# Layer 0: both adjacency mixes side by side, then both weight stages; each mix emptied by ScalarE and VectorE

## The chip, the cores and the metric

The kernel runs on one core of a Trainium2 chip. The metric is the device time of one execution in microseconds; the figure given is the median of several runs.

## The reference

Input x is 128 graphs of 64 nodes with 256 features, 8192 tokens in all; adj is one 64 by 64 adjacency matrix shared by all graphs. Four layers follow each other, each on a layer norm with a ReLU, each added to x. The change is in the first half of layer 0, two graph convolutions; the LSTM windows after them, and the layers 1 to 3 (attention, a normalised graph convolution, a three-step graph convolution) are not touched.

```python
h = jnp.maximum(_layernorm(x, axis=-1), 0.0)
# layer 0, up to the LSTM
h = relu(einsum('ts,bsh->bth', adj, h @ Wg0 + bg0))
h = relu(einsum('ts,bsh->bth', adj, h @ Wg1 + bg1))
```

## The kernel before

All data are float32. The tokens of layer 0 are worked off in 16 groups (`NG`) of 512 tokens (`GN`), each as four tiles of 128 tokens. The product with adj is taken before the product with the weights, so that a group passes through these stages:

- layer norm (`ln_relu`, L84 to L120): statistics on VectorE (L92, L94, L95), the power -1/2 on GpSimd (L96), a last small step on VectorE (L98), and four ScalarE instructions (L111) that write the normalised tile h.
- the first mix (`first_mix`, L428): 32 small matmuls of 64 by 64 (L145) multiply adj with h, into two PSUM banks. Two copies empty the banks into the tile m0: L158 and L453 are where they are issued.
- the first weights (`first_weights`, L480): 8 matmuls over the full array (L488) multiply m0 with the first weight matrix, into two banks. VectorE adds the bias (L496), GpSimd takes the ReLU (L497); the result is h1.
- the second mix (`second_mix`, L500): again 32 small matmuls (L145), adj with h1, into two banks; two copies (L158) fill m1.
- the second weights (`second_weights`, L505): 4 matmuls over the full array (L512), the weight matrix with m1, into two banks. For each of the two banks VectorE adds the bias (L517) and ScalarE writes the ReLU in a turned layout (L520) to the tile that the LSTM reads.

A matmul of float32 stands in the trace as two records. In the prediction mix1, W1, mix2 and W2 are these four stages on TensorE, T is the start of a mix1, and a number in brackets is a group's.

The groups overlap by a hand-written loop (L523 to L533). In iteration g, TensorE receives the first mix of group g, then the second weights of group g-2, then the second mix of group g-1, then the first weights of group g. In iteration 16 the second weights of group 14 are cut in two around the second mix of group 15. Each engine takes its own instructions in the order in which the tile framework's scheduler wrote them; they wait on each other by semaphores. Except for group 0, both copies of a first mix are on VectorE (`on_vector`, then `on_vector_last`), and both copies of a second mix are on ScalarE, except for the last one, which has one on each. The tiles h, m0, h1, m1 and s1 have two buffers each, x three; PSUM has eight banks, which all matmuls share in turn. `issue_after` puts an instruction behind another in the order: the statistics of a layer norm behind the copy of two groups ahead, its step L98 behind the copy of the group ahead.

The loads of x (L58) and of the LSTM's weights (L319) are issued from SyncE's queue. After the last group the LSTM begins; its matmuls are at L569.

Of the kernel before, what the change touches and what calls it, by code (L numbers as in the profile page):

```python
# [20 lines left out]
NG = NTOK // GN  # L21
# [17 lines left out]
def adj_preln_kernel(ctx: ExitStack, tc: tile.TileContext, x_in, adj, vec, bg0, bg1,  # L39
# [9 lines left out]
    def bank(shape=(P, 512)):  # L49
        return psp.tile(list(shape), F32, tag="ps", name="ps")  # L50
# [6 lines left out]
    def load_x(x, g):  # L57
        nc.sync.dma_start(out=x, in_=x_view[:, g * GT : (g + 1) * GT, :])  # L58
# [13 lines left out]
    adj2 = const.tile([P, NODES], F32, tag="adj2", name="adj2")  # L72
# [44 lines left out]
    def ln_relu(src, dst, between=None):  # L117

        rstd, nmr, _ = ln_scale(src, between)
        ln_apply(src, dst, rstd, nmr)  # L120
# [11 lines left out]
    def mix(src, a2, chunks, dst, copies, swap=False, banks=None, behind=lambda t, last: None,  # L132
            order=None):

        for c0, tiles in order or [(c0, range(GT)) for c0 in range(0, chunks, 2)]:
            pss = banks.pop(0) if banks else [bank((P, 2, GT, NODES)) for _ in range(2)]
            for t in tiles:
                for c in range(2):  # L140
                    for half in range(2):
                        for b in range(2):
                            rows = slice(b * 64, b * 64 + 64)
                            col = (c0 + c) * P + half * 64
                            last = nc.tensor.matmul(  # L145
                                pss[b][half * 64 : half * 64 + 64, c, t, :],
                                lhsT=src[rows, t, col : col + 64],
                                rhs=a2[rows, :],
                                start=True, stop=True,
                            )  # L150
                behind(t, last.ins)
            for b in range(2):
                if swap:
                    to = dst[:, c0 : c0 + 2, :].rearrange("p c (k b m) -> p b c k m", b=2, m=P)
                    last = copies[b](to[:, b], pss[b].rearrange("p c (k q) n -> p c k (q n)", q=2))
                else:
                    to = dst[:, c0 : c0 + 2, :].rearrange("p c (t b n) -> p b c t n", b=2, n=NODES)
                    last = copies[b](to[:, b], pss[b])  # L158
        return last.ins

    on_vector, on_scalar = nc.vector.tensor_copy, nc.scalar.copy
# [153 lines left out]
    with tc.tile_pool(name="lw", bufs=5) as lw:  # L315
# [6 lines left out]
        with tc.tile_pool(name="gw", bufs=1) as gw, tc.tile_pool(name="gcn", bufs=2) as gp, \  # L322
# [105 lines left out]
            def first_mix(g):  # L428
                nonlocal first_copied, first_scalar, turned, second_ln
                h = gp.tile([P, GT, D], F32, tag="h", name="h")  # L430
                if g == 0:
                    for k, (rstd, nmr, _) in enumerate(lns):
                        two = slice(2 * k, 2 * k + 2)
                        ln_apply(xs[0][:, two], h[:, two], rstd, nmr, 2, (1,) if k else ())
                elif g == 1:
                    with tc.issue_after(first_copied):
                        rstd, nmr, second_ln = ln_scale(xs[1])
                    with tc.issue_after(first_scalar):
                        ln_apply(xs[1], h, rstd, nmr)
                    with tc.issue_after(first_copied):  # L440
                        row_sums()
                else:
                    if g < NK:
                        x = xs[g]
                    else:
                        x = gp.tile([P, GT, D], F32, tag="x", name="x", bufs=3)
                        load_x(x, g)
                    with tc.issue_after(second_ln if g == 2 else copied_of[g - 2].ins):
                        ln_relu(x, h, lambda: copied_of[g - 1])
                m0 = gp.tile([P, 2, GN], F32, tag="m0", name="m0")  # L450

                def on_vector_last(*args):
                    copied_of.append(nc.vector.tensor_copy(*args))  # L453
                    return copied_of[-1]

                if g == 0:


                    def on_scalar_first(*args):
                        nonlocal first_scalar  # L460
                        last = nc.scalar.copy(*args)
                        first_scalar = last.ins
                        return last

                    copied = mix(h, adj2, 2, m0, (on_scalar_first, on_vector_last))
                    first_copied = copied
                    with tc.issue_after(copied):
                        nc.vector.tensor_scalar(rb0[:, 0, :], rb0[:, 0, :], rsum, None, ALU.mult)
                else:
                    copied = mix(h, adj2, 2, m0, (on_vector, on_vector_last))  # L470
                if g == NG // 4:

                    with tc.issue_after(copied):
                        adjacency_forms()
                        turned = normalized_adjacency()
                if g == NG // 2:
                    turned()
                return m0

            def first_weights(m0):  # L480

                h1 = gp.tile([P, GT, D], F32, tag="h1", name="h1")
                for k in range(2):
                    ps = bank((P, 2, D))
                    for t in range(2):
                        tok = (2 * k + t) * P
                        for c in range(2):
                            nc.tensor.matmul(  # L488
                                ps[:, t, :],
                                lhsT=m0[:, c, tok : tok + P],  # L490
                                rhs=wg[0][:, c, :],
                                start=(c == 0),
                                stop=(c == 1),
                            )
                    hk = h1[:, 2 * k : 2 * k + 2, :]
                    nc.vector.tensor_tensor(hk, ps, rb0.to_broadcast([P, 2, D]), ALU.add)  # L496
                    nc.gpsimd.tensor_scalar(hk, hk, 0.0, None, ALU.max)  # L497
                return h1

            def second_mix(h1, last):  # L500
                m1 = gp.tile([P, 2, GN], F32, tag="m1", name="m1")
                mix(h1, adj2, 2, m1, (on_scalar, on_vector if last else on_scalar))
                return m1

            def second_weights(g, m1, ms=range(2)):  # L505

                dst = hs[g // PER][:, :, :, (g % PER) * GB : (g % PER + 1) * GB]
                for m in ms:
                    ps = bank((P, GB, NODES))
                    pf = ps.rearrange("p b n -> p (b n)")  # L510
                    for c in range(2):
                        nc.tensor.matmul(  # L512
                            pf, lhsT=wg[1][:, c, m * P : (m + 1) * P], rhs=m1[:, c, :],
                            start=(c == 0), stop=(c == 1),
                        )
                    s1 = gp.tile([P, GB, NODES], F32, tag="s1", name="s1")
                    nc.vector.tensor_tensor(  # L517
                        s1, ps, rb1[:, m].to_broadcast([P, GB, NODES]), ALU.add
                    )
                    nc.scalar.activation(dst[:, m], s1.rearrange("p b n -> p n b"), AF.Relu)  # L520


            h1, m1 = None, None  # L523
            for g in range(NG + 2):
                if g < NG:
                    m0 = first_mix(g)
                before = m1
                if before is not None:
                    second_weights(g - 2, before, range(1 if g == NG else 2))
                m1 = second_mix(h1, g == NG) if h1 is not None else None  # L530
                if g == NG:
                    second_weights(g - 2, before, [1])
                h1 = first_weights(m0) if g < NG else None  # L533


        with tc.tile_pool(name="back", bufs=1, reuse_waits="tile") as back_pool, \
# [198 lines left out]
            for p, nk in ((1, 8), (2, 8), (3, 7), (4, 8)):  # L735
# [7 lines left out]
                for j in range(0, len(units), 2):  # L743
# [23 lines left out]
                    for t in range(1, p):  # L767
                        for i, u in enumerate(two):
# [21 lines left out]
                            if p == 4 and j == 2 and t == p - 1 and i == 0:  # L790

                                h = back_pool.tile([P, GT, D], F32, tag="hc", name="h")
# [59 lines left out]
    with tc.tile_pool(name="att", bufs=2, reuse_waits="tile") as ap_:  # L852
# [150 lines left out]
        last, put_down = None, None  # L1003
        for g in range(NG):
# [14 lines left out]
            if g == 0:  # L1019
                h = normalized(1)  # L1020
# [50 lines left out]
            last = (e_next[0], ri_next, v)  # L1071
            with tc.issue_after(sub):
# [4 lines left out]
                if g + 2 < NG:  # L1077
                    h = normalized(g + 2)
# [155 lines left out]
    for g in range(NG):  # L1234
# [20 lines left out]
        else:  # L1255
# [11 lines left out]
            def evicted(m):  # L1267
                return nc.scalar.copy(o[:, m, :], pss[m])

            for m in range(2):  # L1270
                nc.vector.bn_stats(st2[:, m, g, :], pss[m])
                if (g, m) != (NG - 1, 1):
                    last = evicted(m)
# [302 lines left out]
    for g in range(NG + 1):  # L1576
        if g == 0:
            bring(0, 3)
        if g < NG:

            m1 = arena(ar_right)
            h1, summed = first_weights(a, m1)
# [91 lines left out]
```

## Time and profile before

| what | value |
|---|---|
| median of 3 runs | 2445.6 us (2445.13 to 2445.6) |
| profiled execution: its time, its span | 2446.36 us, 2444.5 us |
| TensorE busy | 2425.3 us (99%) |
| VectorE, ScalarE, GpSimd busy | 1539.8, 1127.5, 463.9 us |
| granted TensorE clock | 0.999 |
| first matmul of the LSTM | starts at 162.96 us |

A profile shows one execution. Its busy times are sums over each engine, PE is TensorE's matmuls and PEld its weight loads, DVE is VectorE, ACT ScalarE, POOL GpSimd, SP SyncE. A line's bracket at its end gives the idle time of the engine before that instruction, and what ended it; "issue" is time in which it waited for nothing that the profile shows. L numbers are lines of the kernel's file. What happens up to 163 us is layer 0's two graph convolutions, 7% of the span; the rest is not part of the change.

### The profile page before, as it was taken

The page shows a single profiled execution, that of the slowest core. Times are in us where ns is not written, and L with a number is a line of the kernel's source. Part 1 is how long each engine was busy: PE and PEld are TensorE (multiplying, and loading weights), DVE is VectorE, ACT ScalarE, POOL GpSimd, SP SyncE. Part 2 cuts the span into 40 slices and gives each one's busy share as a digit, 9 for nine tenths or more (in the row PEclk, how much of TensorE's full clock was granted, in tenths as well). Part 3 has the DMA queues.
Part 4 walks back from the last instruction along what each step waited for, and adds up shares of the span by engine and source line. Part 5 has one row for each costly group of instructions (what it writes and reads, how often), then busy time and mean ns, then how long its engine had stood idle before and what let it go on. Part 6 is the DMA issues. An engine that isn't in the chain of part 4 may idle for free.

```text
span 2444.5 us, 46563 instructions
## 1 busy us (share of the span) xinstructions
PE 2425.3 (99%) x19564; PEld 2068.5 (85%) x19564; DVE 1539.8 (63%) x2752; ACT 1127.5 (46%) x2010; POOL 463.9 (19%) x400
## 2 busy tenths in 40 slices
PE   9999999999999999999999999999999999999999
PEld 6678888889999998888888864486988898898888
DVE  6668866666566675575599886476556445454544
ACT  4557754544444443353455566564333323333332
POOL 4432211111111111112224431023111111101110
PEclk9999999999999999999999999999999999999999
DMA  3200000001000000143246410010133100000000
GB/s 128 94 2 1 1 18 1 1 1 35 1 1 1 1 1 1 18 96 70 48 81 128 79 36 2 1 61 10 29 60 62 27 10 19 10 10 10 18 10 18
DMA packets 161585, 73.20 MB, mean 30 GB/s; under 512 B 104416, under 2 KB 157792, under 8 KB 161376
## 3 DMA queue, kind: packets, MB, share of 16 engines
q1 hardware_dynamic: 147712, 56.82, 9.5%
q0 software_dynamic: 12672, 12.58, 3.4%
q8 instruction: 154, 2.52, 0.4%
q10 hardware_dynamic: 992, 0.82, 0.1%
q14 instruction: 55, 0.45, 0.1%
HBM read 40.84 MB, written 20.97 MB: 25 GB/s over the span
## 4 chain that ended last, share of the span: by engine, by line
PE 91%; DVE 5%; ACT 2%; issue 1%; DMA 0%; POOL 0%; DVEq 0%; ACTq 0%; POOLq 0%
PE ps L569 41%; PE ps L1459 16%; PE ps L1507 8%; PE ps L831 4%; PE ps L1419 4%; PE ps L145 4%; PE ps L881 3%; PE ps L512 2%; PE ps L488 2%; PE ps L1211 2%; PE ps L1262 2%; PE ps L903 1%; PE ps L1528 1%; PE ps L964 1%; DVE e L947 1%
## 5 line engine op out<-in xcount | busy, mean ns | idle before, releaser
L569 PE MATMUL ps<-diff,s 128*128 128x256 f32 (+1 forms) x1824 | 393.5, 371 | 0.9 <-DVE diff L690 0.9
L1459 PE MATMUL ps<-arena 128*128 128x256 f32 x1792 | 393.3, 380 | 0.3 <-DVE arena L215 0.3
L1459 PEld LDWEIGHTS ps<-arena 128*128 128x128 f32 x1792 | 337.9, 190 | 55.1 <-issue 9.8
L569 PEld LDWEIGHTS ps<-diff,s 128*128 128x128 f32 x1824 | 345.9, 190 | 33.8 <-issue 1.6
L583 ACT ACTIVATE gates<-gates,lbias 128x512 f32<-128x512 f32 (+5 forms) x426 | 244.3, 621 | 200.5 <-DVE gates L194 144.4
L188 POOL TENSOR_TENSOR gates<-p 128x512 f32<-128x512 f32 (+1 forms) x115 | 148.6, 1292 | 882.0 <-DVE p L184 831.1
L569 PE MATMUL ps<-h,w 128*128 128x256 f32 (+1 forms) x1028 | 241.0, 371 | 0.0
L569 PE MATMUL ps<-diff,w 128*128 128x256 f32 (+1 forms) x1040 | 238.7, 370 | 0.0
L569 PEld LDWEIGHTS ps<-diff,w 128*128 128x128 f32 x1040 | 197.4, 190 | 18.2
L569 PEld LDWEIGHTS ps<-h,w 128*128 128x128 f32 x1028 | 195.0, 190 | 19.2 <-issue 0.5
L583 ACT ACTIVATE gates<-ps,lbias 128x256 f32<-128x256 f32 (+3 forms) x213 | 91.9, 477 | 247.5 <-PE ps L569 247.4
L188 POOL TENSOR_TENSOR arena<-arena 128x256 f32<-128x256 f32 (+1 forms) x73 | 82.2, 1126 | 579.0 <-DVE arena L184 549.3
L238 ACT ACTIVATE arena<-arena 128x512 f32<-128x512 f32 x144 | 88.1, 627 | 187.0 <-POOL arena L188 95.0
L1507 PE MATMUL ps<-arena 128*128 128x128 f32 x1280 | 149.7, 276 | 0.0
L194 DVE TENSOR_TENSOR gates<-p,ps 128x512 f32<-128x512 f32 (+1 forms) x115 | 76.4, 664 | 114.4 <-PE ps L569 114.2
L1507 PEld LDWEIGHTS ps<-arena 128*128 128x128 f32 x1280 | 145.5, 192 | 1.1
L194 DVE TENSOR_TENSOR arena<-arena,ps 128x256 f32<-128x256 f32 (+1 forms) x73 | 43.6, 597 | 156.2 <-PE ps L1459 87.4
L183 DVE TENSOR_TENSOR p<-p,ps 128x512 f32<-128x512 f32 (+1 forms) x131 | 86.9, 663 | 47.9 <-PE ps L569 46.7
L569 PE MATMUL ps<-state,w 128*128 128x256 f32 (+1 forms) x512 | 116.1, 370 | 0.9 <-ACT p L180 0.8
L198 DVE TENSOR_TENSOR gates<-p,ps 128x512 f32<-128x512 f32 (+1 forms) x115 | 76.6, 666 | 63.3 <-PE ps L569 62.7
L831 PE MATMUL ps<-arena,w 128*128 128x512 f32 x256 | 116.0, 606 | 0.0
L569 PE MATMUL ps<-state,s 128*128 128x256 f32 (+1 forms) x512 | 115.8, 369 | 0.0
(207 smaller groups left out, 4012.0 us busy)
## 6 DMA issues: line engine op xcount, KB each, us to landing
x<-in_x SPq DMA_DIRECT2D x19, 512.0 KB, 4.2
y<-turned SPq DMA_DIRECT2D x64, 128.0 KB, 3.6
v<-vt SPq DMA_DIRECT2D x128, 64.0 KB, 2.3
w<-in_wih SPq DMA_DIRECT2D x4, 1024.0 KB, 7.6
x_for_h<-in_x SPq DMA_DIRECT2D x8, 512.0 KB, 7.1
x<-y POOLq DMA_DIRECT2D x8, 512.0 KB, 6.3
x_for_h<-y POOLq DMA_DIRECT2D x8, 512.0 KB, 6.7
z<-w SPq DMA_DIRECT2D x64, 64.0 KB, 2.0
```

Source lines behind the costliest of these rows:

```text
L145: last = nc.tensor.matmul(pss[b][half * 64 : half * 64 + 64, c, t, :], lhsT=src[rows, t, col : col + 64], rhs=a2[rows, :], start=True, sto ...
L183: nc.vector.tensor_tensor(p1, p1, ps[2], ALU.add)
L188: nc.gpsimd.tensor_tensor(out=out[1][1], in0=p1, in1=p5, op=ALU.add).ins
L194: nc.vector.tensor_tensor(out[0][1], p1, ps[1], ALU.add)
L198: last = nc.vector.tensor_tensor(to, p, q, ALU.add)
L238: nc.scalar.activation(o, o, func)
L569: nc.tensor.matmul(ps[:, r], lhsT=wc[:, j, :], rhs=bc, start=first and r == 0 and c == 0, stop=True, skip_group_check=True,)
L583: nc.scalar.activation(o, ps, func, bias=lbias[:, col : col + 1])
L831: nc.tensor.matmul(ps, lhsT=w1[:, c, m * P : (m + 1) * P], rhs=a[:, 2 + c, :], start=(c == 0), stop=(c == 1),)
L1419: nc.tensor.matmul(ps[:, t, :], lhsT=w[:, t * P : (t + 1) * P], rhs=b, start=first and t == 0, stop=True, skip_group_check=True,)
L1459: nc.tensor.matmul(ps[:, r, :], lhsT=w[:, c, col : col + P], rhs=b[:, c, :], start=first and r == 0 and c == 0, stop=c == 1, skip_group_ch ...
L1507: nc.tensor.matmul(ps[:, t, :], lhsT=w[:, c, t * P : (t + 1) * P], rhs=b[:, c, :], start=first and t == 0 and c == 0, stop=c == 3, skip_gr ...
```

## The change

Three things are done. The loop is written anew: in iteration g TensorE receives the first mix of group g, the second mix of group g-1, the first weights of group g, and the second weights of group g-1; there are 17 iterations where there were 18. The first of the two copies of a first mix moves from VectorE to ScalarE. The second of the two copies of a second mix moves from ScalarE to VectorE, in every group. The special case in iteration 16 goes.

```diff
-                    copied = mix(h, adj2, 2, m0, (on_vector, on_vector_last))
+                    copied = mix(h, adj2, 2, m0, (on_scalar, on_vector_last))
...
-            def second_mix(h1, last):
+            def second_mix(h1):
                 m1 = gp.tile([P, 2, GN], F32, tag="m1", name="m1")
-                mix(h1, adj2, 2, m1, (on_scalar, on_vector if last else on_scalar))
+                mix(h1, adj2, 2, m1, (on_scalar, on_vector))
                 return m1
 
-            def second_weights(g, m1, ms=range(2)):
+            def second_weights(g, m1):
...
-                for m in ms:
+                for m in range(2):
...
-            h1, m1 = None, None
-            for g in range(NG + 2):
+            h1 = None
+            for g in range(NG + 1):
                 if g < NG:
                     m0 = first_mix(g)
-                before = m1
-                if before is not None:
-                    second_weights(g - 2, before, range(1 if g == NG else 2))
-                m1 = second_mix(h1, g == NG) if h1 is not None else None
-                if g == NG:
-                    second_weights(g - 2, before, [1])
-                h1 = first_weights(m0) if g < NG else None
+                m1 = second_mix(h1) if g else None
+                if g < NG:
+                    h1 = first_weights(m0)
+                if g:
+                    second_weights(g - 1, m1)
```

## The prediction

> **What bounds the kernel now.** I read the page's busy times first, then the table of stretches over one group of 512 tokens, then the order of time of that group. Columns of the first lines: busy us, share, instructions; of the stretch: length, then busy us and count of PE, PEld, DVE, ACT, POOL.
>
> ```profile
> span 2444.5 us, 46563 instructions
> PE 2425.3 (99%) x19564; PEld 2068.5 (85%) x19564; DVE 1539.8 (63%) x2752; ACT 1127.5 (46%) x2010; POOL 463.9 (19%) x400
> 126.26:135.73 9.47, 9.47 (x153) 6.45 (x153) 6.36 (x17) 5.05 (x8) 4.01 (x4) 1.00 0.01 2
> ```
>
> TensorE is never idle in layer 0's steady stretch. From the first W1 of the steady part (start 18.38) to the last (151.01) there are 14 groups, 132.63 us, so 9.474 each. Time can only come from TensorE's own losses, and is lost wherever a copy comes too late. The order of time of one group (start, us, engine, line; x is the count) shows both:
>
> ```profile
> 127.36 0.30 PEld L512 LDWEIGHTS ps<-m,wg 128*128 128x128 f32 x2
> ...
> 130.41 1.08 ACT L520 ACTIVATE h<-s 128x512 f32<-128x512 f32 x1
> 130.72 0.23 DVE L94 BATCH_NORM_AGGREGATE mv<-st 128x2 f32<-128x6 f32 x2
> 130.99 1.02 PEld L145 LDWEIGHTS ps<-adj,h 64*64 64x64 f32 x64 [0.76 <-issue]
> 130.99 1.16 PE L145 MATMUL ps<-adj,h 64*64 64x64 f32 x64
> 131.16 0.69 DVE L517 TENSOR_TENSOR s<-ps,rb 128x512 f32<-128x512 f32 x1 [0.22 <-PE ps L512]
> ...
> 131.89 1.11 ACT L520 ACTIVATE h<-s 128x512 f32<-128x512 f32 x1
> ...
> 132.08 3.32 PEld L488 LDWEIGHTS ps<-wg,m 128*128 128x128 f32 x16
> 132.08 3.72 PE L488 MATMUL ps<-wg,m 128*128 128x256 f32 x16
> ...
> 132.91 1.06 ACT L158 COPY m<-ps 128x512 f32<-128x512 f32 x2
> ...
> 135.73 1.02 PEld L145 LDWEIGHTS ps<-adj,h 64*64 64x64 f32 x64 [0.33 <-issue]
> 135.73 1.16 PE L145 MATMUL ps<-adj,h 64*64 64x64 f32 x64
> ...
> 136.94 0.69 DVE L158 COPY m<-ps 128x512 f32<-128x512 f32 x1 [0.41 <-PE ps L145]
> 137.55 0.68 DVE L453 COPY m<-ps 128x512 f32<-128x512 f32 x1
> ```
>
> From start to start of the weight loads: W2 (L512) 127.36 to 130.99 = 3.63, mix2 1.09, W1 (L488) 132.08 to 135.73 = 3.65, and mix1 likewise 1.10. The reader is to see what follows each change of tile shape, and that ACT works at 131.89 to 133.97 on things for which TensorE does not wait.
>
> **What the Trainium skill says.** "TensorEngine Tiling (Array Packing)", Key Properties: changing the tiling mode drains the TensorE. The trace agrees. Sixteen full-array W1 records in a long full-array run take 3.45 (layer 0's LSTM, 166.20 to 169.65), but 3.65 when a mix follows: 0.20 per change. A mix's 64 loads span 1.02, of which the last is 0.13: (1.02 - 0.13)/63 = 14.1 ns each, 0.90 in all, against 1.09: 0.19 for the way back. Same page, PSUM Bottleneck: both ScalarE and VectorE should empty PSUM. True only if both are free at that moment. "TensorE: Matmul & The Clock Gate", Step-by-step: TensorE is the only engine that reorders. Then ACT takes its queue in the written order; in this trace ACT's order of time is that order.
>
> **The change, part by part.** (a) TensorE's order per group goes from mix1, W2, mix2, W1 to mix1, mix2, W1, W2. Four changes of shape become two. If nothing else held TensorE, a group would be 9.474 - 0.20 - 0.19 = 9.08, a gain of 0.39.
>
> (b) Before, 3.63 us of W2 lay between mix1 and W1, which reads m0; DVE's two copies (137.55 + 0.68 = mix1 start + 2.50) were covered. Now only mix2 lies between: W1 could start at mix1 start T + 0.90 + 1.09 = T + 1.99. DVE's half of m0 comes at T + 1.21 (136.94 - 135.73) + 0.69 + 0.06 to release TensorE (0.05 at 18.38, 0.10 at 9.25) = T + 1.96: just covered.
>
> (c) ACT's half is the question. In the order built for the changed program ACT has, from the third group to the last, L520, L520, L158 (m0), three L111, L158 (m1), one L111. So the m0 copy stands behind the second L520 of the W2 that has just ended at T. Its chain, link by link from rows of before, where the same instructions follow a W2: L517 starts 0.17 after the next mix starts (131.16 - 130.99); 0.69 long; 0.04 to L520 (0.03 at 151.17); L520 to the next copy 1.00 (131.89 to 132.91 is 1.02, 141.37 to 142.35 is 0.98); ACT's copy 0.58; 0.06 to TensorE. Sum 2.54. It ends 0.55 after the mixes, so W1 waits for it and the saved drains are hidden under that wait. Both ends: 2.50 and 2.62.
>
> (d) W1 and W2 now join: 3.45 + 8 records of W2 at 0.429 (4.29 for ten, 158.24 to 162.53) = 3.43, + 0.20 for the change at the end = 7.08. The last W1 of before, with half a W2 joined to it, confirms it: 151.01 to 156.38 is 5.37 = 3.45 + 1.72 + 0.20. Both ends 7.04 and 7.12.
>
> A group is then 2.54 + 7.08 = 9.62: **+0.146, and 14 of them +2.0** (9.54 to 9.74: +0.9 to +3.7).
>
> (e) First groups: W1 of group 1 waited until 18.38 for DVE's second copy of m0. ACT takes one now, idle there after 16.01; DVE's single copy ends at 17.05 + 0.68 and no longer binds. mix2 ends about 18.11: -0.27 (0 to -0.3).
>
> (f) Tail: before, W2 of group 14 was cut in two around the last mix2, and from W1(15) to the LSTM's first matmul was 162.96 - 151.01 = 11.95. Now W2(14) is whole, and the last W2 has nothing in front of it but mix2 and the same chain through L517, L520, L158: 7.08 + 2.54 + (3.43 + 0.11 for the first load) = 13.16: **+1.2** (0.8 to 1.5).
>
> (g) Moved at no cost: DVE and ACT do as many copies as before (2 and 2 per group), and DVE is at 6.36 of 9.47. m1 must be ready when W1 ends, T + 6.0; ACT's copy, behind three L111 (0.49 each) after the m0 copy, ends near T + 4.5, covered by W1; without that cover W2 would wait. POOL: before, h1's second half is ready 135.73 + 0.30 + 2.4, so 2.4 after W1 ends (126.26, then 127.15 + 1.48 = 128.63). It is needed after W2 and a mix, 3.63 + 0.90 later; even a 1.03 L96 ahead of it stays hidden. DMA: on SP's queue one 1 MB weight load goes in front of one x load (about 56 us); that x is first read some 24 us later against a landing of 4 to 8. PSUM: eight banks per group, as before. After layer 0 the order on TensorE, DVE, ACT and POOL is the same; it only starts later.
>
> Sum: -0.27 + 2.0 + 1.2 = **+3.0**. The profiled execution took 2446.36 with a span of 2444.5, so it would become 2449.3 and 2447.5; it lies 0.76 above the median 2445.6, to which I add: **2448.6**. 0.2%, 4.9 us, is about what a measurement of this kernel can tell from no change.
>
> **Rivals.** *The drains are won* (faster). If the m0 copy is not held by L520, W1 starts at T + 1.99, a group is 9.07: 14 x -0.40 = -5.6; tail, the chain from mix2 alone 1.21 + 0.69 + 0.06: 7.08 + 1.96 + 3.54 - 11.95 = +0.6; head -0.27; together -5.2: 2440.4. For it: shape changes are real and DVE's half is in time. Against: ACT's written order, and 131.89 + 1.00 which is later than the mix by itself. Chance 0.08.
>
> *A longer chain* (slower). One mechanism: L517 starts late. It did once, where two L517 waited with nothing else beside them:
>
> ```profile
> 150.45 0.69 DVE L517 TENSOR_TENSOR s<-ps,rb 128x512 f32<-128x512 f32 x1 [0.78 <-ACT h L520]
> ```
>
> That is 0.53 after the mix's start at 149.92, 0.36 more than usual. Before, it cost nothing; now it would go straight into TensorE. At every group: 14 x 0.51 + 1.6 - 0.27 = +8.4: 2454.0. Two L517 now stand side by side in nearly every group, which speaks for it; that the pair at 138.91 and 140.63 showed no delay speaks against. It decides (over +4.9) once the chain is longer than 2.67. Chance 0.13.
>
> *The change does not do what it says, or gain and wait cancel*: TensorE's built order is as described, so only the second can be: chain 2.40, group 9.48, tail +1: 2446. Chance 0.07. My forecast has the rest, 0.72.
>
> **How the numbers follow.** Forecast alone, with the bounds of (c) to (f): +1.5 to +4.8, so 2447.1 to 2450.4. The range adds the cancelling case and the near part of the longer chain: 2445.4 to 2452.0, leaving out the win and the far end. Faster by over 0.2%: 0.08. Slower by over 0.2%: the longer chain 0.13 and the upper edge of the forecast 0.04. Within: 0.75.
>
> **What would show it.** In the changed profile, in steady groups: L145 runs of two mixes; L488 starting 2.5 after them and PE idle about 0.5 there, released by ACT's m copy; L520 right before that copy; L512 following L488 with no wait; W1 to W1 9.62; the LSTM's first matmul near 166. Wrong if L488 follows the mixes at 2.0, if the released engine is DVE, or if W2 waits for m1 or a mix for h or h1.

## The result, and the profile after

The changed kernel takes 2448.61 us (median), the kernel before 2445.16 us in the runs beside it: a ratio of 1.0013, 95% interval 1.0007 to 1.0019, so 3.45 us slower. 2448.6 was forecast.

The page of the changed kernel, its first lines, and the stretch of one group (length, then busy us and count of PE, PEld, DVE, ACT, POOL, then the granted clock and, last, two figures for DMA):

```profile
span 2447.0 us, 46567 instructions
PE 2422.0 (99%) x19564; PEld 2070.1 (85%) x19564; DVE 1539.4 (63%) x2752; ACT 1128.7 (46%) x2010; POOL 462.9 (19%) x400
132.06:141.70 9.64, 9.18 (x153) 6.43 (x152) 6.28 (x17) 5.13 (x9) 3.96 (x3) 1.00 0.01 2
```

A group now lasts 9.64 us and TensorE works in 9.18 of them: less work than the 9.47 of before, and a hole of 0.46. The same group of the changed kernel in order of time shows the hole:

```profile
132.06 1.96 PEld L145 LDWEIGHTS ps<-adj,h 64*64 64x64 f32 x128 [0.76 <-issue]
132.06 2.10 PE L145 MATMUL ps<-adj,h 64*64 64x64 f32 x128
132.24 0.69 DVE L517 TENSOR_TENSOR s<-ps,rb 128x512 f32<-128x512 f32 x1 [1.02 <-PE ps L512]
132.96 1.13 ACT L520 ACTIVATE h<-s 128x512 f32<-128x512 f32 x1 [0.64 <-DVE s L517]
133.31 0.69 DVE L453 COPY m<-ps 128x512 f32<-128x512 f32 x1 [0.39 <-PE ps L145]
...
134.00 0.57 ACT L158 COPY m<-ps 128x512 f32<-128x512 f32 x1
...
134.62 3.32 PEld L488 LDWEIGHTS ps<-wg,m 128*128 128x128 f32 x16 [0.60 <-ACT m L158]
134.62 3.72 PE L488 MATMUL ps<-wg,m 128*128 128x256 f32 x16 [0.46 <-ACT m L158]
...
137.96 0.41 PEld L512 LDWEIGHTS ps<-m,wg 128*128 128x128 f32 x2
...
141.70 1.96 PEld L145 LDWEIGHTS ps<-adj,h 64*64 64x64 f32 x128 [0.76 <-issue]
```

T is 132.06. Both mixes, mix1 of this group and mix2 of the one before, run as one row of 128 records. VectorE's half of m0 starts at T + 1.25 and is done at T + 1.94; ScalarE begins its half only at T + 1.94, right behind the second ReLU of the W2 that ended at T. W1 starts at T + 2.56, released by ScalarE. W2 follows W1 without a wait. The waits of TensorE in the changed kernel from 18 to 170 us (who waited for whom: us in total, times, longest) hold little else; the kernel before had 0.3 us there in one wait:

```profile
PE ps L488 <- ACT m L158: 5.8, 13, 0.5
PE ps L512 <- ACT m L158: 1.3, 1, 1.3
PE ps L488 <- DVE w L227: 0.5, 1, 0.5
PE ps L145 <- POOL h L497: 0.4, 1, 0.4
```

The first and third lines are the same hole: 14 waits, of W1(2) to W1(15), 6.3 us together. The 0.5 put down to L227 is W1(15); its weight load (at 153.90) is released by ScalarE's copy like the others, and L227 writes a tile that W1 does not read. The second line is the tail: the last W2 has only the last mix2 in front of it. The fourth, the wait for h1 of group 0, stands at 17.42 in the kernel before too.

**Where the time went**, from the two profiled executions (first weight load of W1; in the last column the first LSTM matmul). The head is what lies ahead of W1(1), the tail what follows W1(15):

| us | W1(0) | W1(1) | W1(15) | a group, mean of 14 | LSTM |
|---|---|---|---|---|---|
| before | 9.22 | 18.38 | 151.01 | 9.473 | 162.96 |
| changed | 10.27 | 18.98 | 153.90 | 9.637 | 167.02 |

The LSTM starts 4.06 later. Of these 14 x 0.164 = 2.29 are the steady groups, 13.12 - 11.95 = 1.17 the tail, and 1.05 - 0.45 = 0.60 the head. The 1.05 lies ahead of anything that the change moves: in the eight profiled executions of this document W1(0) starts anywhere between 9.18 and 11.52. Of the 0.45 that is gained from W1(0) to W1(1), the change's part is seen in these lines, of before, then of the changed kernel; the L145 is the second half of mix2(0):

```profile
17.42 0.56 PEld L145 LDWEIGHTS ps<-adj,h 64*64 64x64 f32 x32 [0.57 <-POOL h L497]
17.65 0.68 DVE L453 COPY m<-ps 128x512 f32<-128x512 f32 x1
18.38 3.32 PEld L488 LDWEIGHTS ps<-wg,m 128*128 128x128 f32 x16 [0.40 <-DVE m L453]
```

```profile
17.98 0.68 DVE L453 COPY m<-ps 128x512 f32<-128x512 f32 x1
18.36 0.56 PEld L145 LDWEIGHTS ps<-adj,h 64*64 64x64 f32 x32 [0.57 <-POOL h L497]
18.98 3.32 PEld L488 LDWEIGHTS ps<-wg,m 128*128 128x128 f32 x16
```

From there to W1(1) it takes 0.96 before and 0.62 now, so the change saves 0.34 in the head. The same two values return in the experiments: 0.95 where both copies of m0 are on VectorE, 0.62 or 0.63 in all the others. What lies between W1(0) and this place took 7.6 and 8.1 in two kernels that have the same order there, so the other 0.11 can't be put down to the change.

The spans differ by 2.5 only, because of one spot in layer 2. The matmuls of L831 (L829 in the changed kernel, two lines having gone) in order of time, of before, then of the changed kernel:

```profile
1451.78 8.83 PE L831 MATMUL ps<-arena,w 128*128 128x512 f32 x16
```

```profile
1455.88 7.13 PE L829 MATMUL ps<-arena,w 128*128 128x512 f32 x16
```

Sixteen equal records took 8.83 in the one and 7.13 in the other; in the profile of before the granted clock was 0.56 from 1453 to 1456. The profiled execution of before lost 1.70 there, in a layer that the change does not touch: 4.06 - 1.70 = 2.4. None of the other seven executions lost it: from the LSTM's first matmul to the end they took 2279.4 to 2279.9, and before 2281.5. Groups, tail and head come to 2.29 + 1.17 - 0.34 = 3.1. The medians, which come from many executions, give 3.45, with an interval of 1.7 to 4.6 (0.07% to 0.19%), and agree with that.

### The profile page after: what moved, and what is told of

The parts are those of the page before. It is cut to its first block, busy times and chain, and to the rows that moved or that the text cites. A ratio compares the mean times of both kernels' runs of the same rounds, so it can differ in the third digit from the quotient of the medians.

```text
span 2447.0 us, 46567 instructions
## 1 busy us (share of the span) xinstructions
PE 2422.0 (99%) x19564; PEld 2070.1 (85%) x19564; DVE 1539.4 (63%) x2752; ACT 1128.7 (46%) x2010; POOL 462.9 (19%) x400
## 4 chain that ended last, share of the span: by engine, by line
PE 91%; DVE 6%; ACT 2%; issue 1%; POOL 0%; DVEq 0%; ACTq 0%; POOLq 0%
PE ps L567 41%; PE ps L1457 16%; PE ps L1505 8%; PE ps L1417 4%; PE ps L829 4%; PE ps L145 3%; PE ps L879 3%; PE ps L488 2%; PE ps L512 2%; PE ps L1209 2%; PE ps L1260 2%; PE ps L901 1%; PE ps L1526 1%; PE ps L962 1%; DVE e L945 1%
## 5 line engine op out<-in xcount | busy, mean ns | idle before, releaser
L829 PE MATMUL ps<-arena,w 128*128 128x512 f32 x256 | 114.3, 599 | 0.0
```

The costliest lines, as they stand in the source:

```text
L829: nc.tensor.matmul(ps, lhsT=w1[:, c, m * P : (m + 1) * P], rhs=a[:, 2 + c, :], start=(c == 0), stop=(c == 1),)
```

## The experiments

The theory was that ScalarE's half of m0, queued behind the second ReLU of W2, makes W1 wait and hides what the joined mixes save, the pauses of TensorE at a change of tile shape (the drains of the prediction). The rivals were that another wait stands behind it at once, that the joining saves nothing, and that it is the sharing of the copies, or ScalarE's amount of work, that counts.

**The ReLU behind the copy.** The second ReLU of each W2 is held back until ScalarE has taken its half of the next m0 (in the last iteration, of m1); `scalar_copy` holds ScalarE's last copy. The main lines of the edit:

```diff
-                    nc.scalar.activation(dst[:, m], s1.rearrange("p b n -> p n b"), AF.Relu)
+                    def relu(m=m, s1=s1):
+                        nc.scalar.activation(dst[:, m], s1.rearrange("p b n -> p n b"), AF.Relu)
+                    if m == 0:
+                        relu()
+                return relu
...
+            def relu_behind_copy():
+                if relu is not None:
+                    with tc.issue_after(scalar_copy[0].ins):
+                        relu()
...
                     m0 = first_mix(g)
+                    relu_behind_copy()
                 m1 = second_mix(h1) if g else None
+                if g == NG:
+                    relu_behind_copy()
...
-                    second_weights(g - 1, m1)
+                    relu = second_weights(g - 1, m1)
```

> The changed kernel, but ScalarE takes the second ReLU of a W2 (L520 there) behind its half of the m0 copy, not ahead of it; of the last mix2 likewise. Theory (the m0 copy queued behind that ReLU makes W1 wait, and hides the saved drains): the copy starts when the mix ends, T + 1.25 (the VectorE half does so in the changed kernel), VectorE's half ends at T + 1.94 and releases TensorE at 1.99, the two mixes end at 2.03 (0.94 + 1.09), so W1 starts at T + 2.04 in place of 2.56 and a group is 9.12 in place of 9.64. Against the kernel before: 14 x -0.35 = -5.0, tail 7.08 + 1.99 + 3.54 - 11.95 = +0.7, head -0.3: about -4.6 us, near 2440.6. Rival (another wait takes the ReLU's place at once: VectorE's half, the layer norm or h1 comes late, or the joined mixes save nothing): W1 still 2.5 after the mixes' start and a time of 2446 to 2449.

Measured: 2441.55 against 2445.09 before, ratio 0.9984 (0.9978 to 0.9991): 3.5 us faster than before and 7 faster than the change. A group, in order of time (here L430 is ScalarE's copy, L458 VectorE's, L527 the ReLU, L493 W1), and the stretch of the group in front of it:

```profile
136.16 1.96 PEld L145 LDWEIGHTS ps<-adj,h 64*64 64x64 f32 x128 [0.76 <-issue]
...
137.42 0.69 DVE L458 COPY m<-ps 128x512 f32<-128x512 f32 x1 [0.39 <-PE ps L145]
137.43 0.59 ACT L430 COPY m<-ps 128x512 f32<-128x512 f32 x1 [1.00 <-PE ps L145]
137.91 1.12 ACT L527 ACTIVATE h<-s 128x512 f32<-128x512 f32 x1
...
138.22 1.81 PEld L493 LDWEIGHTS ps<-wg,m 128*128 128x128 f32 x9
138.25 1.97 PE L493 MATMUL ps<-wg,m 128*128 128x256 f32 x8
```

```profile
127.01:136.16 9.15, 9.15 (x153) 6.44 (x153) 6.28 (x17) 5.13 (x9) 3.96 (x3) 1.00 0.01 2
```

Both copies now start together, 0.01 apart, W1 comes at T + 2.06 with no wait listed in front of it, and TensorE is busy for the whole of its 9.15. The theory holds: one place in ScalarE's order, with ScalarE's 5.13 us of work unchanged, decides over 0.49 us in the group shown and 0.47 in the mean of 14. What was a little off is the saving itself: the mean group is 9.168 (three of the 14 last 9.22 to 9.29), so 9.473 - 9.168 = 0.305 are saved per group, where 0.35 was expected.

**The order alone**: TensorE's new order, with the copies where they were before.

```diff
-                    copied = mix(h, adj2, 2, m0, (on_scalar, on_vector_last))
+                    copied = mix(h, adj2, 2, m0, (on_vector, on_vector_last))
...
-                mix(h1, adj2, 2, m1, (on_scalar, on_vector))
+                mix(h1, adj2, 2, m1, (on_scalar, on_scalar))
```

> The new TensorE order alone: both copies of a first mix on VectorE and both of a second mix on ScalarE, as before the change. Theory: VectorE's copies follow each other, T + 1.25 + 0.61 + 0.69 + 0.05 = T + 2.60, so W1 waits for VectorE and a group is 9.68 (14 x +0.21 = +2.9 against before); the last W2 waits for two ScalarE copies behind the ReLU, 0.5 more than in the changed kernel (+1.7 in the tail); head 0. About +4.6 us against before, 2449.8, so 1 us slower than the changed kernel: sharing the copies gained almost nothing, since both halves meet a busy engine. Rival (the ReLU's chain is not what W1 waits for): W1 not released by VectorE, and the time of the changed kernel or below.

Measured: 2449.06, ratio to before 1.0016 (1.0009 to 1.0022), 4.0 us slower than before. A group of it, in order of time:

```profile
131.49 1.96 PEld L145 LDWEIGHTS ps<-adj,h 64*64 64x64 f32 x128 [0.76 <-issue]
...
132.70 0.69 DVE L158 COPY m<-ps 128x512 f32<-128x512 f32 x1 [0.34 <-PE ps L145]
133.31 0.68 DVE L453 COPY m<-ps 128x512 f32<-128x512 f32 x1
134.04 2.02 PEld L488 LDWEIGHTS ps<-wg,m 128*128 128x128 f32 x10 [0.60 <-DVE m L453]
```

W1 comes at T + 2.55, released by VectorE's second copy: the same hole, by another engine. The groups are 9.645 each, 0.01 longer than in the change, and the tail 13.61, 0.5 longer. So in the changed kernel the sharing of the copies brought almost nothing in the groups; two halves one behind the other on VectorE, and one half behind a ReLU on ScalarE, happen to end at the same time. Once the ReLU is out of the way, the sharing does count: W1 comes at T + 2.06 in the first experiment, and here at T + 2.55, with no ReLU in front of either copy.

**The copies alone**, in TensorE's old order (the two lines of the diff that name the copies, in the kernel before).

> The kernel before with the copies alone changed: one half of each mix on ScalarE and one on VectorE; TensorE's order is that of before. Theory: the copies are covered by 3.6 us of W1 or W2, so a group stays at 9.47 and the time at 2445 (head -0.3). Rival (copies by two engines cost or bring something by themselves, by contention in PSUM or a freer engine): off by over 1 us.

Measured: 2444.78 against 2445.09, ratio 0.9998 (0.999 to 1.0006). The groups are 9.473 and the tail 11.95, as before. The copies by themselves do nothing where W1 or W2 covers them. In the head, where nothing does, they save the whole 0.34 (W1(1) 0.62 after the second half of mix2(0)); the medians, 0.3 apart, don't resolve it.

**The tail cut again.** On top of the first experiment, the second half of W2(14) stands between the last mix2 and the last W2.

```diff
+                before = m1
                 m1 = second_mix(h1) if g else None
+                if g == NG:
+                    relu = second_weights(g - 2, before, [1])
+                    relu()
...
-                    relu = second_weights(g - 1, m1)
+                    relu = second_weights(g - 1, m1, range(1 if g == NG - 1 else 2))
```

> The kernel of the first run here, and in the last iteration the second half of W2(14) stands between the last mix2 and the last W2, as before the change. Theory: in the tail the wait for m1 is covered again by 1.7 us of W2, so from W1(15) to the LSTM it takes 11.95 as before: 0.7 less than the first run; about -5.3 us against before, near 2439.9. Rival: the tail's wait is not on the path to the end (the LSTM waits for something else), and nothing changes against the first run.

Measured: 2440.85, ratio to before 0.9983 (0.9976 to 0.9990). In the trace the tail is 11.95 again (146.88 to 158.83), where the first experiment has 12.69 (147.37 to 160.06). TensorE's waits from 18 to 170 us in this kernel are down to one, for h1 of group 0 at the start (L502 is GpSimd's ReLU here):

```profile
PE ps L145 <- POOL h L502: 0.4, 1, 0.4
```

The 0.7 us is seen in the trace; the medians (2440.85 and 2441.55) point the same way, but their intervals overlap. This kernel has the lowest median of all, 4.2 us below the one before; 5.3 were expected. Of the difference 0.6 is the groups, which save 0.305 each here too, and not 0.35.

**The ReLU twice, ahead of the copy.** One ScalarE instruction more per group in the changed kernel.

```diff
                     nc.scalar.activation(dst[:, m], s1.rearrange("p b n -> p n b"), AF.Relu)
+                    if m == 1:
+                        nc.scalar.activation(dst[:, m], s1.rearrange("p b n -> p n b"), AF.Relu)
```

> The changed kernel with one instruction more per group: the second ReLU of each W2 (128x512, ScalarE, 1.0 us to the next instruction) is issued twice, to the same place. In the changed kernel ScalarE is busy for half of a group only. Theory (this ReLU stands on the chain from the end of W2 to the next W1): each extra one goes into TensorE in full, W1 at T + 3.56, a group 10.64, 14 x 1.0 + 1.0 in the tail = +15 us against the changed kernel, near 2463.5. Rival (W1 waits for something else, and ScalarE has slack): under +3 us.

Measured: 2466.94, ratio to before 1.0086 (1.0070 to 1.0103), so 18.3 above the changed kernel. In order of time (L522 is the extra ReLU):

```profile
144.99 1.13 ACT L520 ACTIVATE h<-s 128x512 f32<-128x512 f32 x1 [0.64 <-DVE s L517]
...
146.15 1.08 ACT L522 ACTIVATE h<-s 128x512 f32<-128x512 f32 x1
147.13 0.57 ACT L158 COPY m<-ps 128x512 f32<-128x512 f32 x1
...
147.75 0.30 PEld L488 LDWEIGHTS ps<-wg,m 128*128 128x128 f32 x2 [1.71 <-ACT m L158]
```

The extra ReLU starts 1.16 after the first (both write the same place; whether that is the reason was not tried) and the copy 0.98 after it: the group grows by 1.11 in place of 1.0, 14 x 1.11 = 15.5. The tail grows by 2.8, of which 1.1 is the ReLU; for the rest see the last section. The chain goes into TensorE in full.

**The ReLU twice, behind the copy.** The same extra instruction in the kernel of the first experiment.

```diff
                     def relu(m=m, s1=s1):
                         nc.scalar.activation(dst[:, m], s1.rearrange("p b n -> p n b"), AF.Relu)
+                        if m == 1:
+                            nc.scalar.activation(dst[:, m], s1.rearrange("p b n -> p n b"), AF.Relu)
```

> The same extra ReLU in the kernel where the second ReLU stands behind the m0 copy; the order on ScalarE is then copy m0, ReLU, a layer-norm part, the extra ReLU, a layer-norm part, copy m1, two layer-norm parts. Theory: off the chain it is hidden. The m1 copy comes about 0.5 later than without it, near T + 5.3, and W2 asks for m1 at T + 5.4; so 0 to +1 us against 2441.5. Rival (what counts is ScalarE's amount of work, not its place): +14 us as in the other kernel.

Measured: 2441.39, ratio to before 0.9983 (0.9975 to 0.9990), against 2441.55 without the extra one; groups 9.168 as without it. In order of time (lines as in the first experiment; L529 is the extra ReLU):

```profile
125.95 1.96 PEld L145 LDWEIGHTS ps<-adj,h 64*64 64x64 f32 x128 [0.76 <-issue]
...
127.17 0.59 ACT L430 COPY m<-ps 128x512 f32<-128x512 f32 x1 [0.93 <-PE ps L145]
...
127.65 1.10 ACT L527 ACTIVATE h<-s 128x512 f32<-128x512 f32 x1
...
128.02 3.10 PEld L493 LDWEIGHTS ps<-wg,m 128*128 128x128 f32 x15
...
129.14 1.08 ACT L529 ACTIVATE h<-s 128x512 f32<-128x512 f32 x1
```

W1 comes at T + 2.07, before either ReLU is through. The same work costs 18 us ahead of the copy and nothing behind it: it is the place, not the amount.

## Why the prediction was right, point by point

- **The total.** The mechanism came out as forecast, in place and size. That the figure 2448.6 was met to the digit is luck: the prediction added 3.0 to a median of 2445.6 from three runs, and in the runs beside the changed kernel the kernel before took 2445.16 and the change added 3.45. The prediction also took 4.9 us for the least that can be told from no change; here the interval of 1.7 to 4.6 tells 3.45 from it.
- **The chain (c)** was 2.54 by the rows of before and is 2.56: L517 at T + 0.18, L520 0.72 later, the copy 1.04 after it (1.00 was taken), W1 0.62 later (0.64 was taken).
- **W1 and W2 joined (d)**: 7.08 was forecast and is 7.08 (134.62 to 141.70).
- **A group**: 9.62 forecast, 9.637 measured, 14 of them +2.3 for +2.0. **The tail (f)**: 13.16 forecast, 13.12 measured.
- **The head (e)** came out as described: with one copy of m0 on ScalarE, W1(1) no longer waits for VectorE. It saves 0.34, where 0.27 was forecast. The LSTM's first matmul still came at 167.02 and not near 166, because W1(0) began 1.05 later.
- **The saved drains (a), (b)**: right in kind, too large in size. In the first experiment the pair of mixes takes 2.06 to W1 and not 1.99, so 0.305 are saved per group and not 0.39 or 0.40. Not all that is missing need be the drains. There the matmul of W1 starts 0.03 after its weight load (138.25 and 138.22), as in W1(0) of before (9.25 and 9.22), where the profile names VectorE's copy as the last wait of the matmul; in steady groups of before both start together. VectorE's half ends at T + 1.95, so it may still hold W1 by some hundredths, and "just covered" in (b) is not shown. No run tells the two apart. In the changed kernel this didn't matter, as it lies under the wait; the rival that wins the drains would have been given 2440.4, and the first experiment, which is that rival made true, gave 2441.6.
- **What was to stay hidden (g)** did: m1 was ready (ScalarE's second copy at 135.95 to 136.52, W2's load at 137.96), and neither h nor h1 was waited for in a steady group.
- The slower rival, a late L517 in every group, did not occur: the second L517 of a W2 starts 0.11 to 0.18 after the start of the mixes that follow, in all 15 places.
- Slips in the working that change nothing: the sixteen records behind 3.45 are the LSTM's (L569), not W1's; the stray 0.30 in (g) belongs to no sum, 135.73 + 2.4 is meant; the upper ends of (c) to (f), even with the head at -0.3, add up to +4.9, not +4.8; and W1 was to start 2.5 after the start of the mixes, not after the mixes.

The Trainium skill's "TensorEngine Tiling (Array Packing)", Key Properties, says that changing the mode drains the array; taken away and not hidden, two changes were worth 0.305 us per group here, with the doubt named above. Its advice in PSUM Bottleneck to use both engines held here only with the right order in their queues: 7 us lay between the same two copies with the ReLU ahead of one and behind it.

## What to carry to other kernels

Joining stages on TensorE takes away the work that stood between a result and its use, so the copy between them has to be timed anew: follow what its engine still holds in front of it, in the written order of the queue, and not the engine's share of busy time. A row of the trace in which the same two instructions already follow each other gives the price. When such a wait eats a real gain, moving the instruction in front behind the copy may be the whole remedy.

## What the runs showed of the hardware

The clock of TensorE made differences of 1 to 2 us between profiled executions. In the changed kernel W1(0) began at about half speed: nine weight loads took 3.49, against 1.81 before (first lines of W1 of before, then of the changed kernel). The granted clock of the profile reads 1.00 for the stretch from 10.27 to 13.76 all the same, so the half speed is read from the loads alone.

```profile
9.22 1.81 PEld L488 LDWEIGHTS ps<-wg,m 128*128 128x128 f32 x9 [0.99 <-ACT m L461]
```

```profile
10.27 3.49 PEld L488 LDWEIGHTS ps<-wg,m 128*128 128x128 f32 x9 [1.04 <-ACT m L461]
```

With the ReLU twice, the last W2 waited 2.42 us for its copy, and then eight records of it took 5.40 in place of 3.70. The matmuls in order of time, and the stretch with its granted clock:

```profile
179.94 5.40 PE L512 MATMUL ps<-m,wg 128*128 128x512 f32 x8 [2.42 <-ACT m L158]
```

```profile
180.80:184.20 3.40, 3.40 (x5) 1.33 (x4) 0.69 (x1) 0.44 (x1) 0.00 (x0) 0.50 0.00 0
```

That is the 1.7 us of its tail that the ReLU doesn't explain. In the changed kernel a wait of 1.34 at the same place was followed by no such stretch, and with the order alone one of 1.82 neither. Whether the long wait brings the half clock was not tried. It can't be the only way to it: the stretch in layer 2 of before (0.50 from 1452.22 to 1455.63) had no longer wait just ahead of it than one of 1.09, which the changed kernel has at the same place without it.
